# A gated mixture-of-experts kernel on Trainium2: router normalization of later rows moved behind the gate's additions, bias sums of the second layer moved behind the last anchor product

## The chip, the cores and the metric

The kernel runs on one core of one Trainium2 chip. Its engines work side by side, each through its own queue in order: TensorE (PE; PEld is its weight load), VectorE (DVE), ScalarE (ACT), GpSimd (POOL), and SyncE (SP), which issues DMAs. They are kept in step by semaphores. The metric is the device time of one execution in microseconds, given as the median of several runs.

## The reference

The input x has 8 rows of 512 tokens with 256 features; each row has a condition vector and a context of 64 vectors. All is in float32. Cut to what matters:

```python
nx = layer_norm(x)                                     # 8 x 512 x 256
weights = softmax((nx @ Wq) @ (ctx @ Wk).T / 16)       # 8 x 512 x 64
evidence = weights @ (ctx @ Wv)
combined = concat([nx, evidence, anchor])              # 768 features; anchor is the row's condition
router_probs = softmax(combined @ router_W + router_b) # 3 experts
h = silu(combined @ e_w1 + e_b1)                       # 3 experts x 512
routed = sum over e of (h[e] @ e_w2[e] + e_b2[e]) * router_probs[e]
g = sigmoid(silu(combined @ gate_w1 + gate_b1) @ gate_w2 + gate_b2)
out = x + g * (routed @ out_w + out_b)
```

## The kernel before

The eight rows are worked through in four pairs, j = 0 to 3. For each pair the first layer is computed for seven groups of 256 outputs: group 0 is the gate, groups 1 to 6 are the three experts, two groups to an expert. The part of the first layer that multiplies nx is a block product of two feature halves, two output halves and two rows; it is done with seven products in place of eight (`nx_product`, numbers 1 to 7, line 835) and with sums that are formed of the weights (`combine_weights`) and of nx (`combine_x`). The evidence part has the first-layer weights folded into the values (`value_weights`, tile `vw`), so that it becomes products of 64 contexts by 512 tokens (`evidence`, line 795), of which two run side by side in the two halves of the array. The anchor part is the same for all tokens of a row, so it is a bias: `anchor_rows(g)` (line 425) multiplies the conditions with the anchor weights in tiles of 32 columns, DVE transposes the result, and `anchor_columns(g)` adds it to the bias `abias`.

The second layer has the output projection folded in: `second_layer(e)` multiplies e_w2 with out_w into `w2o`. `second_bias` (line 510) does the same for the second layer's biases: products of `ow_sb` and `b2T` in tiles of 32 columns (L517), a transpose out of PSUM, a copy, two subtractions and an addition on DVE (L522 to L528). The result `b2o` is first read in the pair's output stage.

The order on each engine is the order in which the code issues the instructions: it is written by hand. For each pair the driver loop at the end fills two tables of steps with `put`, `within` for the first layers and `between` for the output stage, and `gate_layer`, `expert_layer` and `outputs` call `run` at named points. In `expert_layer` the points are S, W, A, B, C and D, in this order; in `outputs` they are begin, gate, P1, P5, P6, P2, P7, P3 and P4. A step at "gate end" stands in `gate_layer` between the gate's first addition and its evidence products; a step at (0, "S") stands at the beginning of the first expert's layer, right behind the gate's last additions. A PSUM bank of small uses is taken in turn from a list (`spares`, `misc`).

The gate's additions (`add`, line 825, L827) join on DVE what has been copied out of PSUM with a partial sum that is still there. The first, of `ps_u`, must have read the bank before the evidence products write into it again; then come those of `ps_y`, `ps_z` and `ps_w`.

The router: for pairs 1 to 3 the logits and their exponentials are formed in the output stage of the pair before. `router(j)` (line 725) sums the exponentials over the experts (L728), takes the reciprocal (L730) and multiplies (L731), all on DVE and small. `spread_probabilities(j)` (line 736) transposes the result on DVE (L740), writes it to DRAM with four DMAs from POOL's queue (L743), and a fifth, L747, reads it back to all 128 partitions, 1.5 MB, as the tile `pb`. `weigh` (L872) multiplies hidden activations with `pb`; for pairs 1 to 3 it first does so in the second expert's layer.

In the output stage `finish` adds and gates a block of the result on DVE (L1094, L1095), transposes it (L1096), adds x on POOL (L1097) and stores it.

Of the kernel before, what the change touches and what calls it, by code (L numbers as in the profile page):

```python
# [16 lines left out]
def kernel(  # L17
# [53 lines left out]
    B, T, H = x.shape  # L71
# [46 lines left out]
    def load_table(func):  # L118
        nc.scalar.activation(warm_t, warm_t, func)
# [19 lines left out]
    def load_x(b):  # L139
        x_sb[b] = xpool.tile([P, NT, H], F32, tag="x", name=f"x_{b}")  # L140
        j, a = b // 2, b % 2
        if j == 0:
            nc.sync.dma_start(x_sb[b], x[b].rearrange("(t p) d -> p t d", p=P))
            return
        for i, h in SIDES:
            nc.sync.dma_start(x_sb[b][side(i, h), :, :], tile_rows(x[2 * j + i], a, h))
# [5 lines left out]
    def rows_of(w):  # L152
        return w.rearrange("(k p) n -> p k n", p=P)
# [65 lines left out]
    def load_first(g):  # L219
        src, n = (e_w1[g], RH) if g < E else (gate_w1, H)  # L220
        cs = slice(g * RH, g * RH + n)
        nc.sync.dma_start(w1[:, KH:, cs], rows_of(src[H : 2 * H, :]))
        nc.sync.dma_start(w1[:, :KH, cs], rows_of(src[:H, :]))

    def load_anchor(g):
        src = e_w1[g] if g < E else gate_w1
        nc.sync.dma_start(wa[g], rows_of(src[anchor, :]))
# [62 lines left out]
    def wake(n):  # L290

        if not ps_wake:
            ps_wake.append(misc("ps_wake"))
        for _ in range(n):
            nc.tensor.matmul(ps_wake[0][:, :P], zeros, zeros, start=True, stop=True)
# [185 lines left out]
    def load_second(e):  # L481
        load_blocks(w2[e], e_w2[e])
# [48 lines left out]
    S = {}  # L531
# [672 lines left out]
    with tc.manual_schedule(engines=None):  # L1204
        ctx_rows = context.flatten_outer_dims().rearrange("(t p) d -> p t d", p=P)
        for d in range(2):
            half = slice(d * NX // 2, (d + 1) * NX // 2)
            nc.sync.dma_start(ctx_sb[:, half, :], ctx_rows[:, half, :])
        for w_sb, w in ((wk_sb, Wk), (wq_sb, Wq)):
            nc.scalar.dma_start(w_sb, rows_of(w))  # L1210
        nc.sync.dma_start(wv_sb, rows_of(Wv))
        load_table(AF.Sqrt)
        load_x(0)
        load_x(1)
        for g in (E, 0):
            load_first(g)
            load_anchor(g)
        for g in (1, 2):
            load_first(g)

        wake(7)
        context_transposes()
        transpose_weights(wkT, wk_sb, "wk")
        transpose_weights(wqT, wq_sb, "wq")
        statistics(0, 0, NT)
        deviation(0, 0)
        normalize(0)
        project(wv_sb, ctxT, keep_v, "v", (0,))
        join_keys()
        project(wv_sb, ctxT, keep_v, "v", (1,))  # L1230
        statistics(1, 0, NT // 2)
        small_transposes()
        statistics(1, NT // 2, NT)
        transpose_x(0)
        deviation(0, 1)
        router_anchor()
        normalize(1)
        load_table(AF.Exp)
        project(wkqT, ctxT, keep_m, "m")
        value_weights(0, E)  # L1240
        store_router_rows(0)
        combine_weights(E)
        transpose_x(1)
        combine_x(0, nc.vector, (0, 1))
        scores(0)
        load_table(AF.Silu)
        combine_weights(0)
        spread_router_bias()
        spread_router_rows(0)
        softmax(0)  # L1250
        value_weights(0, 0, nc.vector.tensor_copy)
        anchor_rows(E)
        anchor_rows(0)
        combine_x(0, nc.vector, (2,))
        turn_weights(0)
        combine_x(0, nc.vector, (3,))
        combine_weights(1)
        combine_weights(2)
        late_scratch()
        load_anchor(1)  # L1260
        load_anchor(2)
        nc.sync.dma_start(ow_sb, rows_of(out_w))
        nc.sync.dma_start(gw2_sb, rows_of(gate_w2))
        combine_gate()
        load_second(0)

        for j in range(NP):


            within, between = {}, {}  # L1270

            def put(where, n, step, *args):
                where.setdefault(n, []).append(lambda: step(*args))

            if j == 0:
                put(within, "gate", value_weights, 0, 1)
                put(within, (0, "A"), anchor_rows, 1)
                put(within, (0, "A"), router_logits, 0)
                put(within, (0, "A"), load_second, 1)
                put(within, (0, "B"), second_bias)  # L1280
                put(within, (0, "C"), transpose_second, 0)
                put(within, (0, "C"), anchor_columns, 1)
                put(within, (0, "C"), anchor_rows, 2)
                put(within, (0, "C"), router_exp, 0)
                put(within, (0, "D"), router, 0)
                put(within, (0, "C"), load_second, 2)
                put(within, (0, "D"), second_layer, 0)
                put(within, (0, "D"), spread_probabilities, 0)
                put(within, (0, "D"), combine_second, 0)
                put(within, (1, "A"), transpose_second, 1)  # L1290
                put(within, (1, "B"), second_layer, 1)
                put(within, (1, "B"), combine_second, 1)
                put(within, (1, "C"), transpose_second, 2)
                put(within, (1, "C"), anchor_columns, 2)
                put(within, (1, "D"), second_layer, 2)
                put(within, (1, "D"), combine_second, 2)
            if j:
                put(within, "gate end", spread_probabilities, j)
            if j and j + 1 < NP:
                put(within, (0, "B"), statistics, 2 * j + 3, 0, NT)  # L1300
            put(within, (0, "C" if j == 0 else "B"), value_weights, j, 2)
            put(within, (1, "C"), load_x_blocks, 2 * j)
            put(within, (2, "A"), gate_differences, j)
            put(within, (2, "C"), load_x_blocks, 2 * j + 1)
            if j + 1 < NP:
                b0, b1 = 2 * j + 2, 2 * j + 3
                if j == 0:
                    put(within, "gate", load_x, b0)
                    put(within, "gate", load_x, b1)
                if j + 2 < NP:  # L1310
                    put(between, "begin", load_x, b0 + 2)
                    put(between, "begin", load_x, b1 + 2)
                put(within, (0, "A" if j else "D"), statistics, b0, 0, NT)
                if j == 0:
                    put(within, (0, "D"), statistics, b1, 0, NT)
                for i in range(2):
                    put(within, (0, "D") if j else (1, "S"), deviation, j + 1, i)
                for b in (b0, b1):
                    put(within, (1, "W" if j else "S"), normalize, b)
                    put(within, (1, "W" if j else "S"), store_x, b)  # L1320
                put(within, (1, "C"), regroup_x, b0)
                put(within, (1, "A" if j else "B"), router_part, b0)
                put(within, (1, "D" if j else "B"), router_part, b1)
                put(between, "begin", transpose_blocks, b0)
                put(between, "gate", regroup_x, b1)
                put(between, "begin", value_weights, j + 1, E)
                put(between, "begin", store_router_rows, j + 1)
                put(between, "begin", spread_router_rows, j + 1)
                put(between, "P5", transpose_blocks, b1)
                put(between, "P2", scores, j + 1)  # L1330
                put(between, "P2", combine_x, j + 1, nc.gpsimd)
                put(between, "P7", softmax, j + 1)
                put(between, "P7", value_weights, j + 1, 0)
                put(between, "P7", router_logits, j + 1)
                put(between, "P3", value_weights, j + 1, 1)
                put(between, "P3", turn_weights, j + 1)
                put(between, "P3", router_exp, j + 1)
                put(between, "P4", router, j + 1)
            gate_layer(j, within)
            for e in range(E):  # L1340
                expert_layer(j, e, within)
            outputs(j, between)
# [34 lines left out]
```

## The time and profile before

| what | us |
|---|---|
| median of 3 runs (467.15 to 467.54) | 467.28 |
| the profiled execution, whole time | 467.23 |
| its span, first to last instruction | 465.2 |
| addition of products in SBUF, 128x512 (L872), mean of 96 | 0.693 |
| addition of a sum in PSUM, 128x512 (L827, ps_y), mean of 24 | 0.683 |
| addition of x on POOL (L1097), mean of 14 | 1.314 |
| router's product (L731), shortest, median and longest of 4 | 0.182, 1.046, 1.050 |
| landing of pb (L747), median of 4 | 6.5 |

The profile is of one execution. Busy times and means come from its page; a timeline lists instructions by start and duration, and in square brackets how long the engine was idle before and what ended that. The output stage of pair 0 ends near 150 us; pairs 1, 2 and 3 follow at distances of about 106.5 us (their first evidence product starts at 151.75, 258.18 and 364.68).

### The profile page before, as it was taken

Reading aid. Unit: us, or ns where it says so; the run is one execution under the profiler, and the core shown is the slowest. Engines: PE = TensorE matmul, PEld = TensorE weight load, DVE = VectorE, ACT = ScalarE, POOL = GpSimd, SP = SyncE. Lnnn points to the kernel's source line nnn. Section 1 sums busy time; section 2 is a strip of 40 time slices with the busy share of each in tenths; the row PEclk is TensorE's granted clock in tenths of the full one; section 3 lists DMA queues with packets and bytes.
Section 4 is the critical chain, followed back from the end, with each engine's and each line's share of the span. In section 5 each row is a group of like instructions: output and inputs, shape, how many; then the busy total and the mean of one; then the engine's idle time right before and its main releaser. Section 6 shows DMA issues by size and latency. Waiting matters only on the chain.

```text
span 465.2 us, 4763 instructions
## 1 busy us (share of the span) xinstructions
PE 459.4 (99%) x1473; PEld 210.0 (45%) x1473; DVE 363.8 (78%) x672; ACT 214.2 (46%) x369; POOL 95.8 (21%) x133
## 2 busy tenths in 40 slices
PE   9999999999999999999999999999999999999996
PEld 7544555444444344444444344444444344444454
DVE  2994879969799659879799659978889625797973
ACT  3435583655222566557221576448220456458000
POOL 6537224101081300001072300001062300000020
PEclk9999999999999999999999999999999999999999
DMA  9987877403012406813011424702011480000013
GB/s 276 282 160 135 119 232 117 106 0 47 5 23 45 133 29 131 152 35 46 6 24 26 91 87 103 122 3 46 7 23 23 74 200 0 0 0 1 0 22 69
DMA packets 119352, 34.87 MB, mean 75 GB/s; under 512 B 106060, under 2 KB 116352, under 8 KB 118816
## 3 DMA queue, kind: packets, MB, share of 16 engines
q1 hardware_dynamic: 115168, 26.95, 30.0%
q0 software_dynamic: 2128, 6.78, 4.9%
q10 hardware_dynamic: 2032, 0.85, 0.7%
q8 instruction: 11, 0.18, 0.2%
q14 instruction: 13, 0.11, 0.1%
HBM read 27.17 MB, written 7.39 MB: 74 GB/s over the span
## 4 chain that ended last, share of the span: by engine, by line
PE 74%; DVE 19%; issue 3%; DMA 2%; POOL 0%; DVEq 0%; POOLq 0%
PE ps_u L788 34%; PE ps_z L788 14%; PE ps_y L788 12%; DVE h L1064 5%; PE ps_vw L763 3%; PE ps_gu L788 3%; PE ps_w2o L494 2%; DVE r L1095 2%; DVE yb L1096 2%; DVE r L1094 2%; PE ps_gz L788 1%; DMA scr_small<-in_L_xcond_router_W_dram 1%; DVE wT L691 1%; DMA scr_small<-in_L_xcond_e_b_dram 1%; DVE pv L701 1%
## 5 line engine op out<-in xcount | busy, mean ns | idle before, releaser
L872 DVE TENSOR_TENSOR h<-h,pb 128x512 f32<-128x512 f32 x96 | 61.9, 693 | 6.5 <-ACT h L821 6.5
L788 PE MATMUL ps_u<-h,w2o 128*128 128x512 f32 x144 | 64.1, 594 | 0.0
L788 PE MATMUL ps_u<-nxT,w 128*128 128x512 f32 x112 | 55.6, 607 | 0.0
L821 ACT ACTIVATE h<-h,abias 128x512 f32<-128x512 f32 x72 | 49.6, 719 | 13.1 <-DVE h L827 12.6
L788 PE MATMUL ps_z<-wT,vw 64*128 64x512 f32 x104 | 49.5, 605 | 0.0
L1097 POOL TENSOR_TENSOR yb<-yb,xb 128x512 f32<-128x512 f32 x14 | 18.4, 1314 | 148.5 <-DVE yb L1096 120.8
L788 PE MATMUL ps_z<-h,w2s 128*128 128x512 f32 x96 | 42.6, 593 | 0.2 <-DVE r L1080 0.2
L788 PEld LDWEIGHTS ps_u<-h,w2o 128*128 128x128 f32 x144 | 27.0, 190 | 32.5 <-issue 29.2
L830 ACT COPY h<-ps_u 128x512 f32<-128x512 f32 x48 | 28.0, 583 | 28.6 <-PE ps_u L788 26.2
L1064 DVE TENSOR_TENSOR h<-h,h 128x1024 f32<-128x1024 f32 x24 | 34.3, 1482 | 0.0
L408 POOL DMA_DIRECT2D vrd<-vw x8 | 5.0, 629 | 140.3 <-ACT vw L770 140.3
L827 DVE TENSOR_TENSOR h<-h,ps_y 128x512 f32<-128x512 f32 x24 | 16.4, 683 | 21.9 <-PE ps_y L788 21.9
L788 PEld LDWEIGHTS ps_u<-nxT,w 128*128 128x128 f32 x112 | 19.9, 189 | 29.8 <-issue 24.9
L821 ACT ACTIVATE h<-ps_u,abias 128x512 f32<-128x512 f32 x24 | 16.5, 687 | 29.7 <-PE ps_z L788 29.4
L788 PEld LDWEIGHTS ps_z<-h,w2s 128*128 128x128 f32 x96 | 18.1, 190 | 23.5 <-issue 21.8
L788 PE MATMUL ps_u<-wT,vw 64*128 64x512 f32 x56 | 28.2, 617 | 0.5 <-DVE hg L827 0.4
L788 PE MATMUL ps_z<-T,ws 128*128 128x512 f32 x56 | 28.6, 592 | 0.0
L788 PE MATMUL ps_y<-nxT,w 128*128 128x512 f32 x56 | 28.6, 592 | 0.0
L788 PE MATMUL ps_y<-wT,vw 64*128 64x512 f32 x56 | 27.0, 596 | 0.0
L827 DVE TENSOR_TENSOR h<-h,ps_z 128x512 f32<-128x512 f32 x24 | 16.2, 684 | 13.8 <-PE ps_z L788 13.7
L763 PE MATMUL ps_vw<-w,vT 128*128 128x512 f32 (+1 forms) x64 | 26.9, 542 | 0.0
L788 PE MATMUL ps_u<-T,ws 128*128 128x512 f32 x56 | 26.7, 594 | 0.0
(241 smaller groups left out, 798.7 us busy)
## 6 DMA issues: line engine op xcount, KB each, us to landing
pb<-pd POOLq DMA_DIRECT2D x4, 1536.0 KB, 6.5
xb<-in_x_dram SPq DMA_DIRECT2D x64, 64.0 KB, 2.4
out_dram<-yb SPq DMA_DIRECT2D x56, 64.0 KB, 2.0
w<-in_L_xcond_e_w_dram SPq DMA_DIRECT2D x6, 512.0 KB, 9.2
x<-in_x_dram SPq DMA_DIRECT2D x24, 128.0 KB, 3.3
xd<-x SPq DMA_DIRECT2D x24, 128.0 KB, 2.3
xg<-xd SPq DMA_DIRECT2D x48, 64.0 KB, 2.3
scr_wa<-in_L_xcond_e_w_dram SPq DMA_DIRECT2D x3, 512.0 KB, 15.8
```

The lines of the kernel that those rows point to most:

```text
L494: nc.tensor.matmul(ps[:, d * H : (d + 1) * H], w2T[:, k, (i + d) * P : (i + d + 1) * P], ow_sb[:, k, :], start=(k == 0), stop=(k == KH - 1),)
L763: nc.tensor.matmul(ps, vT[:, k, j * 2 * CT : (j + 1) * 2 * CT], w1[:, KH + k, n0:n1], start=(k == 0), stop=(k == KH - 1),)
L788: nc.tensor.matmul(ps, lhsT, rhs, start=start, stop=True, skip_group_check=not start)
L821: nc.scalar.activation(h, h if src is None else src, AF.Silu, bias=abias[:, c, 2 * j + i : 2 * j + i + 1])
L827: nc.vector.tensor_tensor(h, h, part, ALU.add)
L830: nc.scalar.copy(chunk(n, i, d), part)
L872: nc.vector.tensor_tensor(h, h, S["pb", j][:, i, :, 2 * q // RC, :], ALU.mult)
L1064: nc.vector.tensor_tensor(d, p, m, ALU.subtract)
L1094: nc.vector.tensor_tensor(r, r, ps, ALU.add)
L1095: nc.vector.tensor_tensor(r, r, S["hg", row, i], ALU.mult)
L1096: nc.vector.transpose(yb, r)
L1097: nc.gpsimd.tensor_tensor(yb, yb, S["xb", 2 * j + row][:, i, :], ALU.add)
```

## The change

Two steps are put at other points of the hand-written order; no operation is added or removed, and no shape changes.

- `second_bias`, in the first expert's layer of pair 0, moves from point B to point C, behind `anchor_rows(2)`. Point C lies behind the two nx products number 7 and the additions that follow them.
- `router(j)` for pairs 1 to 3 moves from P4, the last point of the pair before, and `spread_probabilities(j)` moves from "gate end"; both now stand at (0, "S").

```diff
@@ -1277,10 +1277,10 @@
                 put(within, (0, "A"), anchor_rows, 1)
                 put(within, (0, "A"), router_logits, 0)
                 put(within, (0, "A"), load_second, 1)
-                put(within, (0, "B"), second_bias)
                 put(within, (0, "C"), transpose_second, 0)
                 put(within, (0, "C"), anchor_columns, 1)
                 put(within, (0, "C"), anchor_rows, 2)
+                put(within, (0, "C"), second_bias)
                 put(within, (0, "C"), router_exp, 0)
                 put(within, (0, "D"), router, 0)
                 put(within, (0, "C"), load_second, 2)
@@ -1295,7 +1295,8 @@
                 put(within, (1, "D"), second_layer, 2)
                 put(within, (1, "D"), combine_second, 2)
             if j:
-                put(within, "gate end", spread_probabilities, j)
+                put(within, (0, "S"), router, j)
+                put(within, (0, "S"), spread_probabilities, j)
             if j and j + 1 < NP:
                 put(within, (0, "B"), statistics, 2 * j + 3, 0, NT)
             put(within, (0, "C" if j == 0 else "B"), value_weights, j, 2)
@@ -1335,7 +1336,6 @@
                 put(between, "P3", value_weights, j + 1, 1)
                 put(between, "P3", turn_weights, j + 1)
                 put(between, "P3", router_exp, j + 1)
-                put(between, "P4", router, j + 1)
             gate_layer(j, within)
             for e in range(E):
                 expert_layer(j, e, within)
```

On DVE the order at the beginning of pairs 1 to 3 was: L728, L730, L731, addition of `ps_u`, L740, additions of `ps_y`, `ps_z`, `ps_w`. It becomes: additions of `ps_u`, `ps_y`, `ps_z`, `ps_w`, L728, L730, L731, L740. The DMAs L743 and L747 keep their places in POOL's queue. On PE, at pair 0, the products of `second_bias` go behind four 128x512 instructions of nx products and the products of `anchor_rows(2)`; on DVE its five operations go behind two additions, two transposes of weights and the work on the anchor.

## The prediction

> **What bounds the kernel now.** I read the busy table first, then the waits of TensorE's weight loads, then the order of events at the start of one later pair of rows (j=1), and last the same place at j=0, which serves as a control.
>
> ```profile
> span 465.2 us, 4763 instructions
> PE 459.4 (99%) x1473; PEld 210.0 (45%) x1473; DVE 363.8 (78%) x672; ACT 214.2 (46%) x369; POOL 95.8 (21%) x133
> ```
>
> PE (TensorE) is busy 99% of the span, at full clock in all 40 slices. Ends of matmuls are modelled, so small holes are looked for in the starts of weight loads (PEld): in a steady stream of 128x512 products they come every 0.43 us. A time saved on PE is a time saved at the end, as long as nothing late takes it back. The list of waits of the weight loads names two places that the diff touches:
>
> ```profile
> PEld ps_u L788 <- DVE hg L827: 6.3, 8, 1.0
> PEld ps_b2o L517 <- DVE le L704: 0.8, 1, 0.8
> ```
>
> Columns: total us, times, longest. First place, the gate's evidence at j=1, VectorE (DVE) in order of time (start, duration):
>
> ```profile
> 151.11 0.71 DVE L1096 STREAM_TRANSPOSE yb<-r 128x512 f32<-128x512 f32 x1
> 151.75 0.14 DVE L728 TENSOR_REDUCE rsm<-ex 128x8 f32<-128x24 f32 x1
> 151.92 0.20 DVE L730 RECIPROCAL rrs<-rsm 128x8 f32<-128x8 f32 x1
> 152.16 1.05 DVE L731 TENSOR_TENSOR pr<-ex,rrs 128x24 f32<-128x24 f32 x1
> 153.13 0.67 DVE L827 TENSOR_TENSOR hg<-hg,ps_u 128x512 f32<-128x512 f32 x1
> ```
>
> GpSimd (POOL) at that time, from its own timeline:
>
> ```profile
> 151.90 1.26 POOL L1097 TENSOR_TENSOR yb<-yb,xb 128x512 f32<-128x512 f32 x1 [3.76 <-DVE rsm L728]
> ```
>
> and the weight loads:
>
> ```profile
> 152.72 0.19 PEld L788 LDWEIGHTS ps_y<-wT,vw 64*128 64x128 f32 x1 [0.24 <-issue]
> 152.72 0.19 PEld L788 LDWEIGHTS ps_z<-wT,vw 64*128 64x128 f32 x1
> 153.85 0.18 PEld L788 LDWEIGHTS ps_u<-wT,vw 64*128 64x128 f32 x1 [0.94 <-DVE hg L827]
> ```
>
> The reader sees: the router's small product L731 takes 1.05 us, because it stands behind POOL's L1097 until 153.16. Behind it waits the addition L827 that empties bank ps_u, and the evidence products may write ps_u again only after that, at 153.85. At j=0, where no router work stands ahead of the additions, the same load has no extra wait:
>
> ```profile
> 34.22 0.19 PEld L788 LDWEIGHTS ps_u<-wT,vw 64*128 64x128 f32 x1 [0.23 <-DVE hg L827]
> ```
>
> Second place, j=0, the products of second_bias (L517), 32 columns wide, alone between 128-wide ones:
>
> ```profile
> 44.20 0.19 PEld L788 LDWEIGHTS ps_z<-T,ws 128*128 128x128 f32 x1 [0.24 <-issue]
> 45.15 0.27 PEld L517 LDWEIGHTS ps_b2o<-ow_sb,b2T 128*32 128x32 f32 x16 [0.76 <-DVE le L704]
> 45.51 0.30 PEld L788 LDWEIGHTS ps_u<-nxT,w 128*128 128x128 f32 x2
> 46.05 0.19 PEld L788 LDWEIGHTS ps_u<-nxT,w 128*128 128x128 f32 x1 [0.24 <-ACT h L830]
> ```
>
> [...] L731 (two SBUF inputs) takes 1.05 us beside L1097 and 0.18 us at j=0 at 52.47, where POOL is idle; L827 (one input in PSUM) at 58.01 takes 0.69 us although POOL's L233 and L234 run from 57.88 to 59.42. [...]
>
> **The change, part by part.**
>
> *Gate additions ahead of the router (j=1, 2, 3).* From the first evidence load to the first load of the expert layer: at j=0, 32.82 to 36.46, 3.64 us. At j=1, 151.75 to 155.77, 4.02; at j=2, 258.18 to 262.27, 4.09; at j=3, 364.68 to 368.80, 4.12. The excess is 0.38 + 0.45 + 0.48 = 1.31 us. Within j=1: the last product before ps_u starts at 153.15 and takes 0.43, so PE stood from 153.58 to 153.85 (0.27), and the pair after a stall needs 0.54 instead of 0.43 to its second half (0.11), since its weights weren't loaded ahead. After the change the addition may start when L1096 ends (151.82) and the last nx product of ps_u is done (its modelled end is 151.83), say 151.93, and ends at 152.60. The load wants to go at 153.15: spare 0.55 us. So the whole 1.31 us goes. POOL's L1097 runs beside the addition, as it did at 58.01, at no cost.
>
> What is late next: the addition of ps_y needs its evidence (modelled end 152.88) and runs to 153.65; ps_z follows to 154.3; ps_w, whose evidence ends at 154.99 − 0.38 = 154.61, runs from 154.7 to 155.4. Its bank is wanted again for ps_u of the second chunk, at 157.59 − 0.38 = 157.2. Covered.
>
> The router's four operations then cost 0.17 + 0.24 + 0.2 + 0.2 = 0.8 us from their start spacings and end at 156.2. DVE was idle for 3.86 us before 159.58, waiting for ps_y; 3 us remain. Without that cover the 0.8 us would stand in front of the expert layer's first addition.
>
> Later transfers: prT was ready at 153.92, now at 156.2, so 2.3 us later go POOL's four DMAs pd (2.02 us to issue), its pb DMA (158.14) and the memset L581 behind it (158.69), all that POOL has queued there. pb takes 6.5 us to land: 158.7 + 6.5 = 165.2 before, 167.5 after. Its first reader on DVE, L872, comes at 173.23 (j=2: 264.37 to 279.73, j=3: 371.71 to 386.25, alike). The spare shrinks from 8 to 5.5 us: cost nothing. The memset's reader, L590, is at 179.84. SP's queue isn't passed by anything.
>
> *second_bias behind the last anchor product (j=0).* The products stay, and so do five DVE operations, 1.09 us (47.66 to 48.75), which move behind the transpose L438. On PE one switch pair goes: loads at 44.20 and 45.15 are 0.95 apart, against 0.86 for two products, so 0.09; and the first product behind it takes 0.54 (45.51 to 46.05) instead of 0.43, so 0.11. Sum 0.20 us. The anchor products (47.42 to 48.00) have the same 32-column form, so second_bias joins them without a switch. Bounds: 0.36 us if its own issue also hides (all of 45.15 to 45.51), 0 if the two small groups don't follow smoothly. I take 0.20. On DVE the two additions L827 of ps_u and the transposes L486 come 1.09 us earlier; second_layer's products, 0.2 us earlier than 51.11, still find L486 done. Scalar's silus wait for the table load ending at 51.91, not for these additions.
>
> Sum: −1.31 − 0.20 = −1.51 us. Profiled execution: 467.23 us (span 465.2 and 2.0 around it), so 465.7. The median of the runs shown is 467.28, 0.05 above it: 465.75.
>
> Does it survive to the end? In the output stages DVE is backlogged (from 125.6 at j=0 to 153.8), but its chain begins with a PE product, and so starts earlier too; the same holds for the last pair, where DVE's chain to 439.2 starts at PE's product of 421.76.
>
> **The rivals.**
>
> *A, as worked out:* 465.75; 465.3 to 466.3 with 0.5 us for the bounds above, and the 0.4 us between runs.
>
> *B, the additions are held, too.* If L827 waited for POOL until 153.16 as L731 did, it would end at 153.85 and PE would gain nothing at three gates; only 0.20 remains: 467.28 − 0.20 = 467.1. For it: the lock is real, and L1097 starts just there. Against it: L827 at 58.01 beside POOL. The same end comes if the change doesn't reach the order on DVE, but the instruction order shows the additions ahead.
>
> *C, part is taken back.* PE comes earlier to a wait that doesn't follow it (a landing, or a DVE operation that now meets a POOL one: L682 at 138.53 took 1.77 us that way, against 0.69). If half of the gate gain is lost: 467.28 − 0.20 − 0.65 = 466.4. For it: such locks stand in each output stage. Against it: they are released by PE, so they move along.
>
> *D, slower: the probabilities land too late.* One mechanism: pb comes after DVE is ready for L872. It decides from 5.5 us of lateness beyond the 2.3 worked out; then L872 heads DVE's queue with the normalization L549/L552 and the next ps_y addition behind it, and PE waits for these. With 1.5 us beyond that point at each of three pairs: 3 × 1.5 − 1.51 = +3.0, 470.3. [...] Against it: landing lay within 6.4 to 6.6 us in all four cases, and no wait on pb shows.
>
> **How the numbers follow.** A 0.78, B 0.08, C 0.10, D 0.04. What a measurement of this kernel can tell from no change is 0.2%, 0.93 us. Faster: nearly all of A and two thirds of C, 0.84. Same: B, the rest of C, a little of A, 0.12. Slower: D, 0.04. The range takes A and C, leaving B and D out: 465.2 to 466.7.
>
> **What would show it right or wrong.** In the changed profile L731 takes about 0.18 us in all rows, L827 of ps_u starts near 151.9 (less 0.2 for j=0's shift), the ps_u evidence load shows a gap of 0.23 us instead of 0.94 to 1.04, and the four first-to-first distances are all 3.64. second_bias follows the anchor products with no 0.76 gap. L872's wait stays on ScalarE, not on a DMA. If L827 beside L1097 takes over 1 us, B is right; if the distances are 3.64 and the end moves less than 1.2 us, C; if DVE waits for pb, D.

## The result and the profile after

The changed kernel takes 465.87 us (median of 7 runs, 465.67 to 465.97), against 467.26 us before (7 runs, 467.15 to 467.62). The ratio estimated from the runs is 0.9966, with a 95% interval of 0.9956 to 0.9976 (the quotient of the two medians is 0.9970). The forecast was 465.75, within 465.2 to 466.7.

The head of the page, and the chain that ended last:

```profile
span 463.8 us, 4764 instructions
...
PE 457.8 (99%) x1473; PEld 209.8 (45%) x1473; DVE 362.0 (78%) x672; ACT 214.1 (46%) x369; POOL 96.4 (21%) x133
...
PE 93%; DVE 4%; DMA 3%; issue 0%; POOL 0%; POOLq 0%
```

DVE has lost 1.8 us of busy time with the same number of instructions: L731, no longer held, gives 3 × 0.87 = 2.6 us, and other operations took a little more. The chain is now PE for 93% of the span. Before, it ran through DVE for 19%: at pair 1 it led from the evidence load at 153.85 through L827 and L731 back into DVE's work since 125.6.

The gate of pair 1, DVE in order of time (start, duration, instruction):

```profile
150.98 0.71 DVE L1096 STREAM_TRANSPOSE yb<-r 128x512 f32<-128x512 f32 x1
151.74 0.69 DVE L827 TENSOR_TENSOR hg<-hg,ps_u 128x512 f32<-128x512 f32 x1
152.79 0.69 DVE L827 TENSOR_TENSOR hg<-hg,ps_y 128x512 f32<-128x512 f32 x1 [0.37 <-PE ps_z L788]
153.40 0.68 DVE L827 TENSOR_TENSOR hg<-hg,ps_z 128x512 f32<-128x512 f32 x1
154.52 0.69 DVE L827 TENSOR_TENSOR hg<-hg,ps_w 128x512 f32<-128x512 f32 x1 [0.45 <-PE ps_w L788]
155.13 0.17 DVE L728 TENSOR_REDUCE rsm<-ex 128x8 f32<-128x24 f32 x1
155.34 0.20 DVE L730 RECIPROCAL rrs<-rsm 128x8 f32<-128x8 f32 x1
155.57 0.18 DVE L731 TENSOR_TENSOR pr<-ex,rrs 128x24 f32<-128x24 f32 x1
156.11 0.21 DVE L740 STREAM_TRANSPOSE prT<-pr 128x32 f32<-128x32 f32 x1 [0.35 <-DVE pr L731]
```

and POOL at that time:

```profile
151.77 1.26 POOL L1097 TENSOR_TENSOR yb<-yb,xb 128x512 f32<-128x512 f32 x1 [3.76 <-DVE yb L1096]
156.61 2.03 POOL L743 DMA_DIRECT2D pd<-prT  x4 [3.58 <-DVE prT L740]
```

The addition of `ps_u` takes 0.69 us right beside L1097, and DVE now has holes of 0.37 and 0.45 us in which it waits for PE: the roles are exchanged. L731 comes after L1097 has ended and takes 0.18 us. The weight loads of the evidence follow without a hole; that of `ps_u` shows 0.23 us in place of 0.94, and it comes 0.43 us ahead of its product (at 153.45), where before both started at 153.85:

```profile
152.59 0.19 PEld L788 LDWEIGHTS ps_y<-wT,vw 64*128 64x128 f32 x1 [0.24 <-issue]
152.60 0.19 PEld L788 LDWEIGHTS ps_z<-wT,vw 64*128 64x128 f32 x1
153.02 0.19 PEld L788 LDWEIGHTS ps_u<-wT,vw 64*128 64x128 f32 x1 [0.23 <-issue]
```

At pair 0, the weight loads around the bias sums:

```profile
44.41 0.19 PEld L788 LDWEIGHTS ps_z<-T,ws 128*128 128x128 f32 x1 [0.24 <-issue]
44.84 0.19 PEld L788 LDWEIGHTS ps_u<-nxT,w 128*128 128x128 f32 x1 [0.24 <-POOL gw2s L234]
...
47.07 0.38 PEld L433 LDWEIGHTS ps_ar<-scr_wa,condT 128*32 128x32 f32 x16 [0.76 <-DVE h L827]
47.43 0.35 PEld L517 LDWEIGHTS ps_b2o<-ow_sb,b2T 128*32 128x32 f32 x16
47.87 0.30 PEld L763 LDWEIGHTS ps_vw<-w,vT 128*128 128x128 f32 x2
```

L517 has no bracket: it follows L433 at once. The loads that stand at fixed points of PE's program give a ledger of the whole span, in us. The rows "evidence of the gate" reach from a pair's first evidence load to the first load of its expert layer; below they are called the evidence distances.

| stretch of PE's program | before | after | difference |
|---|---|---|---|
| start to the first evidence load, pair 0 | 32.82 | 33.03 | +0.21 |
| evidence of the gate, pair 0 | 3.64 | 3.63 | −0.01 |
| from there to the first `ps_vw` load behind the small groups | 11.54 | 11.21 | −0.33 |
| from there to the evidence of pair 1 | 103.75 | 103.76 | +0.01 |
| evidence of the gate, pair 1 | 4.02 | 3.63 | −0.39 |
| from there to the evidence of pair 2 | 102.41 | 102.41 | 0 |
| evidence of the gate, pair 2 | 4.09 | 3.63 | −0.46 |
| from there to the evidence of pair 3 | 102.41 | 102.41 | 0 |
| evidence of the gate, pair 3 | 4.12 | 3.63 | −0.49 |
| from there to the end | 96.4 | 96.5 | about 0 |

Each row is the difference of two start times. The gains sit in the four places that the change touches, the long stretches between them are the same to 0.01 us, and one loss sits at the start, ahead of anything that was changed.

### The profile page after: what moved, and what is told of

The parts are those of the page before. It is cut to its first block, busy times and chain, and to the rows that moved or that the text cites. A ratio compares the mean times of both kernels' runs of the same rounds, so it can differ in the third digit from the quotient of the medians.

```text
span 463.8 us, 4764 instructions
## 1 busy us (share of the span) xinstructions
PE 457.8 (99%) x1473; PEld 209.8 (45%) x1473; DVE 362.0 (78%) x672; ACT 214.1 (46%) x369; POOL 96.4 (21%) x133
## 4 chain that ended last, share of the span: by engine, by line
PE 93%; DVE 4%; DMA 3%; issue 0%; POOL 0%; POOLq 0%
PE ps_u L788 43%; PE ps_z L788 18%; PE ps_y L788 14%; PE ps_vw L763 5%; PE ps_gu L788 3%; PE ps_w2o L494 2%; PE ps_s L633 2%; PE ps_gz L788 1%; DVE h L1064 1%; DMA scr_small<-in_L_xcond_router_W_dram 1%; DMA scr_small<-in_L_xcond_e_b_dram 1%; PE ps_tokens L788 1%; DVE h L872 1%; PE ps_m L343 1%; PE ps_gy L788 1%; DVE r L1074 0%
## 5 line engine op out<-in xcount | busy, mean ns | idle before, releaser
L872 DVE TENSOR_TENSOR h<-h,pb 128x512 f32<-128x512 f32 x96 | 61.9, 693 | 6.5 <-ACT h L821 6.5
L821 ACT ACTIVATE h<-h,abias 128x512 f32<-128x512 f32 x72 | 49.6, 719 | 11.7 <-DVE h L827 11.2
L1097 POOL TENSOR_TENSOR yb<-yb,xb 128x512 f32<-128x512 f32 x14 | 18.4, 1316 | 144.9 <-DVE yb L1096 129.0
L827 DVE TENSOR_TENSOR h<-h,ps_y 128x512 f32<-128x512 f32 x24 | 16.4, 683 | 19.2 <-PE ps_y L788 15.4
L821 ACT ACTIVATE h<-ps_u,abias 128x512 f32<-128x512 f32 x24 | 16.5, 687 | 29.7 <-PE ps_z L788 29.4
L827 DVE TENSOR_TENSOR h<-h,ps_z 128x512 f32<-128x512 f32 x24 | 16.2, 683 | 14.8 <-PE ps_z L788 14.7
```

The source lines that it names most:

```text
L821: nc.scalar.activation(h, h if src is None else src, AF.Silu, bias=abias[:, c, 2 * j + i : 2 * j + i + 1])
L827: nc.vector.tensor_tensor(h, h, part, ALU.add)
L872: nc.vector.tensor_tensor(h, h, S["pb", j][:, i, :, 2 * q // RC, :], ALU.mult)
L1097: nc.gpsimd.tensor_tensor(yb, yb, S["xb", 2 * j + row][:, i, :], ALU.add)
```

## The experiments

Two questions were open. Is the stall made by the lock (L731 held beside L1097, 1.05 us in place of 0.18), or just by the place of the router in DVE's order, and which addition matters? And how far is the transfer of the probabilities from costing time? The ratios compare each kernel with the kernel before on the same chip.

**Each edit by itself.** Router and spreading as changed, second_bias at its old point:

```diff
-                put(within, "gate end", spread_probabilities, j)
+                put(within, (0, "S"), router, j)
+                put(within, (0, "S"), spread_probabilities, j)
...
-                put(between, "P4", router, j + 1)
```

> Router and spreading behind the gate's additions as in the changed kernel, second_bias at its old point. If the two edits add up (main theory): the distances from first evidence load to first expert load at j=1, 2, 3 all come to 3.63 us, -1.34 us in all, so about 465.95. If the early ledger of the trace is right that second_bias is worth 0.34, this run lies 0.3 above the changed kernel. If the rival holds that part of the gate's gain is lost later (an unmoved wait), it lies above 466.4.

Measured: 465.91 us (465.76 to 466.23), ratio 0.9972 (0.9962 to 0.9983). The three evidence distances are 3.63 us each, 1.34 us less than before, as expected. The 0.3 us between this kernel and the changed one doesn't show in the medians: its start was 32.80 us, that of the changed kernel's profile 33.03. It shows in the trace: from the first expert load to the first `ps_vw` load at pair 0 it takes 11.54 us (36.44 to 47.98), as before.

```diff
-                put(within, (0, "B"), second_bias)
...
+                put(within, (0, "C"), second_bias)
```

> Only second_bias moves. Main theory: one pair of array-mode switches goes and the group's own issue overlaps that of the anchor products; the load at 44.2 to the first ps_vw load takes 3.46 us instead of 3.80, so -0.34 us, about 466.9. The prediction's term was -0.20, so 467.05. Rival (the DVE work behind L438 comes late for second_layer): no gain or a loss, 467.3 or more.

Measured: 467.12 us (467.06 to 467.62), ratio 0.9999 (0.9990 to 1.0007). The time alone tells nothing here. The trace does: from the first expert load at 36.52 to the first `ps_vw` load at 47.72 it takes 11.20 us against 11.54 before, so −0.34, and the evidence distances stay at 4.02, 4.12 and 4.10. So the two edits act in different places and add up.

**The lock taken away, the order kept.** The addition on POOL is left out for the last block of pairs 0 to 2:

```diff
-            nc.gpsimd.tensor_tensor(yb, yb, S["xb", 2 * j + row][:, i, :], ALU.add)
+            if (i, row) != (1, 0):
+                nc.gpsimd.tensor_tensor(yb, yb, S["xb", 2 * j + row][:, i, :], ALU.add)
```

> The order of before, but POOL's addition of x to the last block of pairs 0 to 2 is left out, so that no POOL instruction runs beside the router's product. Theory 1 (the lock makes the stall): L731 takes 0.18 us, the addition of ps_u starts at 152.4 in place of 153.13 and ends before the load wants to go at 153.15; distances 3.64, -1.3 us, about 465.95, with the router still ahead of the additions. Theory 2 (the place in DVE's order alone makes it): the distances stay above 4.0 and the time within 0.2 us of before.

Measured: 465.55 us (465.48 to 465.81), ratio 0.9964 (0.9952 to 0.9977). DVE at pair 1 of this kernel:

```profile
151.66 0.14 DVE L728 TENSOR_REDUCE rsm<-ex 128x8 f32<-128x24 f32 x1
151.84 0.20 DVE L730 RECIPROCAL rrs<-rsm 128x8 f32<-128x8 f32 x1
152.07 0.18 DVE L731 TENSOR_TENSOR pr<-ex,rrs 128x24 f32<-128x24 f32 x1
152.18 0.68 DVE L827 TENSOR_TENSOR hg<-hg,ps_u 128x512 f32<-128x512 f32 x1
```

The router still stands ahead of the addition, yet L731 takes 0.18 us, and the evidence distances are 3.63, 3.64 and 3.64. So the lock was necessary for the stall: without it, three small operations ahead of the addition fit into the spare time. Theory 2 falls. The order mattered because it put an operation that L1097 held (L731, 1.05 us) in front of one that it did not hold (L827, 0.69 us beside it).

The median lies 0.36 us below that of the router's move alone, although the stretches on PE are the same. In the profiles 0.07 of it lies ahead of the last output stage, and the rest between DVE's last addition and the end (463.5 − 460.34 against 463.9 − 460.40). That rest is not explained, and no gain is read from it.

**Only the first addition ahead of the router** (the diff is against the changed kernel).

```diff
-                put(within, (0, "S"), router, j)
-                put(within, (0, "S"), spread_probabilities, j)
+                put(within, "gate end", router, j)
+                put(within, "gate end", spread_probabilities, j)
```

> As the changed kernel, but router and spreading stand behind the first gate addition (ps_u) only, ahead of ps_y, ps_z and ps_w. Theory 1 (only the ps_u addition gates PE): L731 is held by POOL again until 153.0, the other additions come later by about 1 us, the ps_u evidence load keeps its 0.24 gap, distances 3.63, and the time is that of the changed kernel, 465.9. Theory 3 (the later additions gate PE too, through the bank of ps_y, wanted at 155.3): a gap appears at the first expert load and the time rises to 466.2 or more.

Measured: 465.3 us (465.22 to 465.36), ratio 0.9958 (0.9944 to 0.9972). The distances are 3.63 at all three pairs, and from 32.71 on the ledger equals that of the changed kernel. At pair 1:

```profile
151.42 0.69 DVE L827 TENSOR_TENSOR hg<-hg,ps_u 128x512 f32<-128x512 f32 x1
152.47 0.31 DVE L731 TENSOR_TENSOR pr<-ex,rrs 128x24 f32<-128x24 f32 x1
```

L731 takes 0.31 us in place of 0.18: it waits for L1097 again, which ends at 152.74, but PE doesn't wait for what stands behind it. The additions of `ps_y`, `ps_z` and `ps_w` at 152.95, 153.51 and 154.21 come in time. So one addition of the four gates PE, and moving it alone past the router was enough. This order also has prT ready at 153.02, 3.0 us sooner than the changed kernel if the starts are lined up, so it leaves the transfer of the probabilities more room. The lower median isn't a gain of this order: 0.32 us of it is the start, the stretches behind the start are those of the changed kernel, and the rest lies outside the span (465.22 − 463.5 = 1.7 us in its profiled execution, 465.87 − 463.8 = 2.1 in the changed kernel's).

**The changed kernel once more**, to see where its start comes from.

> The changed kernel once more. Its trace gains 1.68 us behind the first 33 us and gives 0.2 to 0.3 back in the start, where router_W lands 0.3 us later. If that start belongs to chance from run to run, the first evidence load comes at 32.8 now and the median near 465.6. If each program has a start of its own, it comes at 33.0 again and the median is 465.9 again.

Measured: 465.71 us (465.66 to 465.95), ratio 0.9965 (0.9951 to 0.9979). The first evidence load comes at 32.78 now. The same program has started at 33.03 and at 32.78, so the 0.21 us of the ledger's first row isn't the change's. The medians, 465.87 and 465.71, differ by less than that, and the kernel before took 467.46 in this series against 467.26: how much of a median is the start is left open.

**Router and spreading later still**, at points A and B of the first expert's layer (the diff, against the changed kernel, is for A; for B the letter alone differs):

```diff
-                put(within, (0, "S"), router, j)
-                put(within, (0, "S"), spread_probabilities, j)
+                put(within, (0, "A"), router, j)
+                put(within, (0, "A"), spread_probabilities, j)
```

> As the changed kernel, with router and spreading another point later, behind the expert layer's first addition of ps_y: prT ready near 160.6 in place of 156.3, pb landed near 171.2, against its first reader at 172.7. Spare of 5.5 us as in the prediction: no wait of L872 on a DMA, same time as the changed kernel within 0.3 us. If the spare is smaller, DVE waits for pb and the time rises.

Measured: 465.8 us (465.63 to 466.1), ratio 0.9966 (0.9952 to 0.9979). prT is ready at 160.43, 4.1 us later than in the changed kernel, and L872 has no wait on a DMA.

> The same at point B: prT near 164.2, pb landed near 174.8, 2.1 us behind its first reader L872. The prediction's slower case (PE waits for what is behind L872 on DVE): up to 2.1 us at each of three pairs, about 472. Rival: DVE's later idle time swallows the 2 us, the wait shows on L872 and the time stays at 465.9.

Measured: 467.68 us (467.38 to 468.07), ratio 1.0005 (0.9997 to 1.0014): 1.97 us more than the changed kernel in the same series. Here the probabilities do come late. DVE at pair 1 of this kernel, then its first readers of `pb` at pairs 2 and 3:

```profile
163.60 0.21 DVE L740 STREAM_TRANSPOSE prT<-pr 128x32 f32<-128x32 f32 x1
...
173.90 2.50 DVE L872 TENSOR_TENSOR h<-h,pb 128x512 f32<-128x512 f32 x4 [1.27 <-DMA pb<-pd]
...
179.93 0.68 DVE L827 TENSOR_TENSOR h<-h,ps_y 128x512 f32<-128x512 f32 x1
```

```profile
280.96 2.50 DVE L872 TENSOR_TENSOR h<-h,pb 128x512 f32<-128x512 f32 x4 [1.64 <-DMA pb<-pd]
```

```profile
389.06 3.10 DVE L872 TENSOR_TENSOR h<-h,pb 128x512 f32<-128x512 f32 x5 [2.67 <-DMA pb<-pd]
```

DVE waits 1.27 + 1.64 + 2.67 = 5.6 us for the transfer. PE loses 0.65 and 1.01 us in the stretches of pairs 1 and 2 (155.09 to 258.15 and 261.79 to 365.21, against 102.41 us each in the ledger), 1.66 us together. That is 0.62 and 0.63 us less than DVE waits, so what stands behind L872 had about 0.6 us to spare. At pair 3 PE loses nothing: no normalization stands behind L872 there, and in the changed kernel DVE is idle for 1.74 and 1.77 us before 389.02 and 392.08, which takes up the wait of 2.67. How lateness reaches PE at pair 1 can be followed through ScalarE:

```profile
180.65 0.72 ACT L821 ACTIVATE h<-h,abias 128x512 f32<-128x512 f32 x1 [1.95 <-DVE h L827]
181.27 0.57 ACT L830 COPY h<-ps_u 128x512 f32<-128x512 f32 x1
```

```profile
181.89 0.30 PEld L788 LDWEIGHTS ps_u<-nxT,w 128*128 128x128 f32 x2 [1.21 <-ACT h L830]
```

With router at point A the same silu L821 started at 179.33. Late L872 makes the addition at 179.93 late, that the silu, that the copy out of `ps_u` queued behind it on ScalarE, and only that holds PE. The expectation of full cost falls; so does its rival of no cost.

**A version below both.** Two edits on top of the changed kernel, not run apart; they act at the two ends of the program, and each is read from its place in the trace: `anchor_rows(1)` joins the other 32-column groups at point C, and in the last pair `keep(r22, z)` goes ahead of the second subtraction.

```diff
-                put(within, (0, "A"), anchor_rows, 1)
...
+                put(within, (0, "C"), anchor_rows, 1)
                 put(within, (0, "C"), anchor_columns, 1)
...
+        if last:
+            keep(r22, z)
         subtract((0, 0), ((0, 1), (0, 0)))
-        keep(r22, z)
+        if not last:
+            keep(r22, z)
```

> The changed kernel with two further edits. First, anchor_rows(1) also goes to point C, so that all three 32-column groups of the first expert's layer stand together: another switch pair goes, -0.2 (the prediction's size of one) to -0.34 us (as measured for second_bias). Second, in the last pair's output stage the addition of ps_z into r22 goes ahead of the second subtraction, so that the ps_z load that comes at 437.75 with a 1.02 gap may go at once: -0.35 to -0.46 us. Together 465.1 to 465.3, against 465.87. Rival: the later anchor transpose delays the bias and the first silus, and DVE's subtractions come late for the next products: no gain.

Measured: 465.07 us (465.0 to 466.01), ratio to before 0.9953 (0.9940 to 0.9965); the changed kernel took 465.71 in this series. Its weight loads at pair 0:

```profile
46.19 0.81 PEld L433 LDWEIGHTS ps_ar<-scr_wa,condT 128*32 128x32 f32 x32 [0.76 <-DMA x<-in_x_dram]
46.98 0.35 PEld L517 LDWEIGHTS ps_b2o<-ow_sb,b2T 128*32 128x32 f32 x16
47.43 0.30 PEld L763 LDWEIGHTS ps_vw<-w,vT 128*128 128x128 f32 x2
```

From the first expert load at 36.55 to `ps_vw` it takes 10.88 us, 0.33 less than in the changed kernel. In the last pair, first the load of the changed kernel that waited, then the loads of this one:

```profile
437.75 0.30 PEld L788 LDWEIGHTS ps_z<-h,w2s 128*128 128x128 f32 x2 [1.02 <-DVE r L1080]
```

```profile
436.11 0.19 PEld L788 LDWEIGHTS ps_u<-h,w2s 128*128 128x128 f32 x1 [0.24 <-issue]
436.54 0.19 PEld L788 LDWEIGHTS ps_z<-h,w2s 128*128 128x128 f32 x1 [0.24 <-issue]
```

From the load of `ps_gu` (415.32) to the end it is 47.58 us against 48.05 (463.8 − 415.75), so −0.47. Both gains are of the size expected, the second at the upper end.

## Why the prediction was right

- **The gate's 1.31 us.** It was taken from the control at pair 0. The ledger gives 1.34, and the three distances are 3.63 where 3.64 was forecast. The mechanism stands by an experiment of its own: with POOL's addition gone the stall went although the order stayed.
- **The addition isn't held beside POOL** (rival B). That of `ps_u` started at 151.74, three hundredths ahead of L1097, and took 0.69 us; L731, which was held, had started 0.26 us behind L1097 (152.16 against 151.90), so this is not the same case. The next one, of `ps_y`, is: it started at 152.79, while L1097 ran from 151.77 to 153.03, and took 0.69 us too (at pairs 2 and 3 likewise, at 258.83 and 364.87). Why L1097 holds L731 and not L827 is not shown by a run. B's 467.1 was not seen.
- **second_bias, the term that was mis-sized.** The sum took 0.20 for one pair of switches (between 128*128 and 128*32) and named 0.36 as the bound if the group's own issue hides, too. It measured 0.33 in the changed kernel and 0.34 by itself. Between wide products the group had cost 0.36 + 0.20 = 0.56 us of PE; behind L433 the two groups together take 0.80 us (47.07 to 47.87) where L433 alone took 0.58 (47.42 to 48.00), so it costs 0.22. The groups overlap: the loads of L517 begin 0.36 us after the first of L433. What makes them overlap is not shown by a run. Nor is the gap in the weight loads the same at each change of the tile's form: in the kernel before, the loads at 45.15 and 47.42, from 128*128 into 128*32, show 0.76 us; on the way back, the load at 48.00 shows 0.20 and that at 45.51 none.
- **The start, a term that was missing.** 0.21 us in the profiled execution stood against the 0.13 more from second_bias and the 0.03 more from the gate, so it is in part luck that the end (−1.40 us of span) lies near the forecast −1.51. The second profile of the same program starts 0.25 us sooner, so the 0.21 is within what varies from one execution to the next.
- **The router's later place.** L728 to L740 end at 156.32 against 156.2 forecast, and DVE still waits 2.75 us for PE before the expert layer's first addition (159.07; 3 us were forecast). L872's wait stays on ScalarE (6.5 us, 5 times, as before).
- **Nothing is taken back** (rival C): the three long stretches are unchanged to 0.01 us.
- **The slower case** (D) was placed rightly and priced too high. The spare was given as 5.5 us. With the two programs lined up at each pair's first evidence load, prT at point B comes 7.7, 8.0 and 8.3 us later than in the changed kernel, and DVE waits 1.27, 1.64 and 2.67 us, so the spare was 6.4, 6.4 and 5.7. Part of the difference is a miscount: the sum added the 6.5 us of landing to the end of L747's issue, but they count from its start (167.45 to L872 at 173.90 is 6.45), which is 0.55 us. Of 5.6 us of waiting, PE felt 1.66 us and the median 1.97, where D had counted each microsecond in full.

## What to carry to other kernels

Where PE waits for a bank to be emptied, look at what stands ahead of that operation in the emptying engine's queue, and move small work that is held by another engine (here L731, 1.05 us in place of 0.18) behind it; check which of several additions is the one that gates (here it was one of four). Where a small operation takes many times what it takes elsewhere in the same trace, look for what holds it, and then for what is queued behind it. When small matmul groups of one array shape stand apart, try them side by side: here it paid twice, 0.33 us each time. And a stage without the suspected cause, if the kernel has one, is a good measure of a stall: here it gave 1.31 us, and 1.34 was measured.

## What was not expected of the hardware

Bringing 32-column groups together saved 0.33 to 0.34 us for each group, twice, which is more than the two holes of a switch (0.09 and 0.11 us) add up to. Where the rest comes from is left open.

The start of the program is set in part by the landing of router_W, a small transfer by POOL. From the profile's chain of waits it took 6.31 us in the kernel before, 6.60 in the changed one and 6.38 with the router alone moved; in the gate-end order's profile the chain runs through the landing of x instead (6.17 us from 2.25). The first evidence load lay between 32.71 and 33.03 us over ten profiles, one program giving both 32.78 and 33.03. An edit worth 0.3 us, such as that of second_bias, is therefore seen in the trace and hardly in the median.
